# A decoder layer on one core: the product with the context is evicted by ScalarE, and a transfer adds the column sums, for seven of eight tiles

## The chip, the cores and the metric

The kernel runs on one core of one Trainium2 chip. The metric is the device time of an execution in microseconds (us). Times of the kernel before were taken in three runs; a further execution was recorded by the hardware profiler, and the views below are of that one. Engines are called as in the profile: PE is TensorE, DVE is VectorE, ACT is ScalarE, POOL is GpSimd, SP is SyncE.

## The reference, cut to what matters

One decoder layer works on 2 x 512 tokens of 1024 numbers: attention inside each token over 32 heads, a product with a context whose both sides are quantised to 256 levels, and a feed-forward part. After each comes an addition of its input and a layer norm.

```python
def _L0_xattn_ref(x1, x2, x1_scale, x1_zp, x2_scale, x2_zp):
    q1 = fake_quant(x1, x1_scale, x1_zp)   # (clip(round(x / s + z), 0, 255) - z) * s
    q2 = fake_quant(x2, x2_scale, x2_zp)
    return jnp.matmul(q1, q2)
...
x = _layernorm(x + _L0_attn_ref(x, Wq, bq, Wk, bk, Wv, bv))
x = _layernorm(x + _L0_xattn_ref(x, ctx_4096, x1_scale, x1_zp, x2_scale, x2_zp))
x = _layernorm(x + _L0_ffn_ref(x, ...))
```

## The kernel before

The 1024 tokens are eight tiles t = 0 to 7 of 128 tokens, one a partition; tile t's tokens lie in `xc` (128 x 1024, f32, in SBUF) and are changed in place. Tiles 0 to 3 use context 0, tiles 4 to 7 context 1. Two tiles make a block of the feed-forward part; blocks 0 and 1 go alone (`ffn`, products `pu` and `pl` at L827, then `pd` at L1057), blocks 2 and 3 together (`ffn_pair`, products `pp` at L942, then `ps` at L1317).

A tile goes through `scores` and `attend`: on DVE four products of 128 x 2048 (L474) with their reductions (L480), the exponentials on ACT (L493), four more products (L507) with reductions (L513), a scaling (L518) and the addition to the tokens with a row sum (L528). Then comes the layer norm. For seven tiles it is `normalise_aside`: ACT turns the row sum into minus the mean (`parts`, L346), takes the sum of squares (L351) and the variance (L353), POOL the reciprocal root `rstd` (L355), and ACT the shift (L359) and the result (L360). Tile 1 is the hurried one: its norms are on DVE (`normalise`: L324, L326, L328, L336) with the root on POOL (L330).

`cross(t, ...)` is the product with the context:

- ACT quantises the tokens in four passes (L375, L378, L381, L644) into `a`, in bf16 as whole numbers; the last pass also gives the row sum `total`. The temporary is `tmp` (tile `qt`, from the pool `work`, three buffers).
- The next tile's `scores` stand between ("between", L648). Then PE turns `a` round (`pta`, L652) and ACT copies it (`aT`, L653). For tile 1 DVE quantises (L364 to L366), and PE turns it at L630.
- Since the quantised numbers are stored from an offset, a row term `r` (from `total`) and a column term `crow` (from the context's column sums, made once a context by PE at L591 and ACT at L594) have to be added: DVE makes `r` (L658) and adds both to `xc` (L659).
- PE makes two products of 128 x 512 (`py`, L665) in two banks, and DVE adds each, scaled by `ns12`, to its half of `xc`, with a row sum (L670). In the up part of `ffn` and ahead of it `py` has banks of `ps_dn`, else of `ps_mm`.
- The layer norm follows, and `hand_over` turns `xc` round on PE (`pt_x`, L134) with copies by ACT (`x2T`, L135); then POOL's queue adds beta to `xc` with a transfer (L737).

Each engine does its instructions in a fixed order. The order comes from a scheduler that lays the steps of two generators (tokens and feed-forward) out with weights (`yield 3.5` and the like). `tc.issue_after(x)` keeps an instruction behind x in that order. `behind()` in `cross` puts DVE's instructions behind the lowering of the next tile's scores (`lowered`, L490), `behind_acted(True)` puts ACT's behind the last eviction of the feed-forward part (`acted`), and `behind_products()` PE's behind its last product (`lately`). `context_beside` quantises context 1 on ACT between the tiles (L375, L378, L577), from loads that POOL's queue issues (L558). In the up part a product `pu` lies in one of two banks of `ps_mm` until ACT has evicted it (L843, then L844), and `pl` likewise (L856, then DVE at L857).

Of the kernel before, what the change touches and what calls it, by code (L numbers as in the profile page):

```python
# [9 lines left out]
F32 = mybir.dt.float32  # L10
BF16 = mybir.dt.bfloat16
AF = mybir.ActivationFunctionType
ALU = mybir.AluOpType
# [3 lines left out]
P = 128  # L17
# [10 lines left out]
def kernel(  # L28
# [24 lines left out]
    nc = tc.nc  # L53
# [18 lines left out]
    HALF = 512  # L72
# [13 lines left out]
    small = ctx.enter_context(tc.tile_pool(name="small", bufs=3))  # L86
# [156 lines left out]
    for k in range(KE):  # L243

        pool, tag = (work, "work") if k % 3 == 0 else (xpool, "xc")
# [37 lines left out]
    with tc.issue_after(added[0].ins):  # L283
# [10 lines left out]
        ns12 = const.tile([P, 1], F32, name="ns12")  # L294
# [3 lines left out]
        s12d2 = const.tile([P, 1], F32, name="s12d2")  # L298
# [34 lines left out]
    def normalise(t, name):  # L333

        mean, rstd = mean_rstd([t[:, ts(h, HALF)] for h in range(E // HALF)], name)
        return nc.vector.tensor_scalar(t, t, mean, rstd, ALU.subtract, ALU.mult)  # L336

    def normalise_aside(t, sums, name):

        n = sums.shape[-1]  # L340
        parts = small.tile([P, 2], F32, tag="parts", name=f"parts_{name}")
        minus = parts[:, 0:1]
        if n > 1:
            minus = small.tile([P, 1], F32, tag="minus", name=f"minus_{name}")
        with behind_acted(True):
            nc.scalar.activation(  # L346
                parts[:, 0:n], sums, AF.Copy, scale=-1.0 / E, accum_out=minus if n > 1 else None
            )
        square = attp.tile([P, E], BF16, tag="square", name=f"square_{name}")
        total = small.tile([P, 1], F32, tag="square", name=f"squares_{name}")  # L350
        nc.scalar.activation(square, t, AF.Square, bias=minus, accum_out=total)  # L351
        ve = small.tile([P, 1], F32, tag="ve", name=f"ve_{name}")
        nc.scalar.activation(ve, total, AF.Identity, scale=1.0 / E, bias=eps)  # L353
        rstd = small.tile([P, 1], F32, tag="rstd", name=f"rstd_{name}")
        nc.gpsimd.tensor_tensor(rstd, ve, neg_half, ALU.pow)  # L355
        yield 3.0
        shift = small.tile([P, 1], F32, tag="shift", name=f"shift_{name}")
        with behind_acted(True):
            nc.scalar.activation(shift, rstd, AF.Identity, scale=minus)  # L359
        return nc.scalar.activation(t, t, AF.Identity, scale=rstd, bias=shift)  # L360

    def quantise(dst, src, tmp, rs, z):

        nc.vector.tensor_scalar(tmp, src, rs, z, ALU.mult, ALU.add)  # L364
        nc.vector.tensor_scalar(tmp, tmp, 0.0, QMAX, ALU.max, ALU.min)
        nc.vector.tensor_scalar(dst, tmp, ROUND, ROUND + CENTRE, ALU.add, ALU.subtract)  # L366

    acted = [None]

    def below_top(dst, src, tmp, rs, z):  # L370

        with behind_acted(dst is None):
            nc.scalar.activation(tmp, src, AF.Relu, scale=rs, bias=z)  # L375
        yield
        with behind_acted(dst is None):
            nc.scalar.activation(tmp, tmp, AF.Identity, bias=round_up)  # L378
        yield
        if dst is not None:  # L380
            nc.scalar.activation(dst, tmp, AF.Relu, scale=-1.0, bias=top_down)  # L381

    def behind_acted(pinned):

        if pinned and acted[0] is not None:
            return tc.issue_after(acted[0].ins)
        return ExitStack()
# [215 lines left out]
    tokens_added, routed = [None], [None]  # L603

    def spare_bank(name):

        if phase[0] in ("front", "up"):
            return ps_dn.tile([P, HALF], F32, tag="dn", name=name)
        return ps_mm.tile([P, HALF], F32, tag="mm", name=name)

    def behind_products():


        return tc.issue_after(lately[0].ins) if lately[0] is not None else ExitStack()

    def cross(t, xc, cq, crow, between):


        hurried = t == TB - 1
        tmp = work.tile([P, E], F32, tag="work", name=f"qt_{t}")  # L620
        a = attp.tile([P, E], BF16, tag="a", name=f"a_{t}")
        aT = tokp.tile([P, KC, P], BF16, tag="aT", name=f"aT_{t}")
        if hurried:

            quantise(a, xc, tmp, rs1, z1)
            yield 2.2
            pt = ps_tr.tile([P, KC, P], BF16, tag="tr", name=f"pta_{t}")
            with behind_products():
                for k in range(KC):
                    codes_turned[0] = nc.tensor.transpose(pt[:, k, :], a[:, ts(k, P)], identb)  # L630
            nc.scalar.copy(aT, pt)
            yield 1.0
            total = ps_tr.tile([P, 2], F32, tag="tr", name=f"pr_{t}")
            with tc.issue_after(expert[0].ins):
                for k in range(KC):
                    nc.tensor.matmul(
                        total, aT[:, k, :], onesb[:, 0:2], start=(k == 0), stop=(k == KC - 1)
                    )
            total = total[:, 0:1]
        else:  # L640
            total = small.tile([P, 1], F32, tag="total", name=f"total_{t}")
            for _ in below_top(tmp, xc, tmp, rs1, z1):
                pass
            nc.scalar.activation(  # L644
                a, tmp, AF.Identity, scale=-1.0, bias=code_down, accum_out=total
            )
            yield 2.0
            yield from between  # L648
            pt = ps_tr.tile([P, KC, P], BF16, tag="tr", name=f"pta_{t}")
            with behind_products():  # L650
                for k in range(KC):
                    nc.tensor.transpose(pt[:, k, :], a[:, ts(k, P)], identb)  # L652
            nc.scalar.copy(aT, pt)  # L653
            yield 4.0
        behind = ExitStack if hurried or t == NT - 1 else lambda: tc.issue_after(lowered[0].ins)
        r = small.tile([P, 1], F32, tag="r", name=f"r_{t}")
        with behind():
            nc.vector.tensor_mul(r, total, s12d2)  # L658
            nc.vector.scalar_tensor_tensor(xc, xc, r, crow, ALU.add, ALU.add)  # L659
        sums = small.tile([P, 2], F32, tag="sum2", name=f"sum2_{t}")  # L660
        for h in range(E // HALF):
            py = spare_bank(f"py_{t}_{h}")
            with behind_products():
                for k in range(KC):
                    crossed[t] = nc.tensor.matmul(  # L665
                        py, aT[:, k, :], cq[:, k, ts(h, HALF)], start=(k == 0), stop=(k == KC - 1)
                    )
            xh = xc[:, ts(h, HALF)]
            with behind():
                tokens_added[0] = nc.vector.scalar_tensor_tensor(  # L670
                    xh, py, ns12, xh, ALU.mult, ALU.add,
                    accum_out=None if hurried else sums[:, h : h + 1],
                )
        if hurried:
            last = normalise(xc, f"2_{t}")
            yield 6.0
        else:
            yield 3.0
            last = yield from normalise_aside(xc, sums, f"2_{t}")
            yield 6.0  # L680
        return last

    def token_path():
# [25 lines left out]
        for blk in range(NBLK):  # L709
            xcs = []  # L710
            x2T = []
            for i in range(TB):
# [9 lines left out]
                if t % (S // P) == 0:  # L722
# [3 lines left out]
                    batch = cqs[b], context_row(b, cqs[b])  # L726
                between = scores_left(t + 1) if t + 1 < NT else ()
                last = yield from cross(t, xc, *batch, between)

                def hand_over(blk=blk, t=t, i=i, xc=xc, x2T=x2T):  # L730
# [756 lines left out]
```

## Time and profile before

| what | before |
|---|---|
| median of three runs | 704.35 us (704.29 to 704.39) |
| the profiled execution | 704.49 us, of which the span from the first to the last instruction is 702.7 us |
| PE busy | 682.4 us, 97% of the span |
| DVE busy | 586.5 us, 83% |
| ACT busy | 261.8 us, 37% |
| POOL busy | 77.0 us, 11% |
| DMA engines, bytes moved | 139.08 MB, mean 198 GB/s |
| granted PE clock | 0.991 of full speed |

The page gives each engine's busy time, cuts the span into 40 slices (17.6 us each) with the busy share of each in tenths, and lists groups of instructions by line, engine, operation and tiles (written<-read), with their count, mean duration and what ended the idle time ahead of them. The view of waits says who waited for whom, in total, how often and longest. The view of one tile or line gives minimum, median and maximum durations in ns and the first and last start in us. The timeline lists instructions in order of time: start, duration, engine, line, operation, and in brackets the idle time ahead of it on its engine and what ended it. The chain of waits goes back from the last instruction to what released each step.

### The profile page before, as it was taken

Reading aid. Unit: us, or ns where it says so; the run is one execution under the profiler, and the core shown is the slowest. Engines: PE = TensorE matmul, PEld = TensorE weight load, DVE = VectorE, ACT = ScalarE, POOL = GpSimd, SP = SyncE. Lnnn points to the kernel's source line nnn. Section 1 sums busy time; section 2 is a strip of 40 time slices with the busy share of each in tenths; the row PEclk is TensorE's granted clock in tenths of the full one; section 3 lists DMA queues with packets and bytes.
Section 4 is the critical chain, followed back from the end, with each engine's and each line's share of the span. In section 5 each row is a group of like instructions: output and inputs, shape, how many; then the busy total and the mean of one; then the engine's idle time right before and its main releaser. Section 6 shows DMA issues by size and latency. Waiting matters only on the chain.

```text
span 702.7 us, 7462 instructions
## 1 busy us (share of the span) xinstructions
PE 682.4 (97%) x2812; PEld 482.6 (69%) x2812; DVE 586.5 (83%) x678; ACT 261.8 (37%) x440; POOL 77.0 (11%) x107
## 2 busy tenths in 40 slices
PE   8999999999999999999999999999999999999991
PEld 4666654578876444478876444488888888888881
DVE  5899987699999999799999950397787688897895
ACT  1287544222635458426736132212251200000252
POOL 1012112100011122001002000020010000001012
PEclk9999999999999999999999999999999999999996
DMA  9999528485446458446436534667897445556733
GB/s 336 304 346 370 127 32 290 116 288 175 135 132 174 178 194 254 134 166 215 145 119 177 182 120 126 238 194 242 338 344 254 164 166 171 168 197 192 207 84 120
DMA packets 70900, 139.08 MB, mean 198 GB/s; under 512 B 5264, under 2 KB 39696, under 8 KB 70864
## 3 DMA queue, kind: packets, MB, share of 16 engines
q1 hardware_dynamic: 60656, 106.87, 44.9%
q0 software_dynamic: 10064, 31.47, 16.3%
q8 instruction: 22, 0.36, 0.2%
q10 hardware_dynamic: 144, 0.26, 0.1%
q14 instruction: 14, 0.11, 0.0%
HBM read 114.99 MB, written 21.50 MB: 194 GB/s over the span
## 4 chain that ended last, share of the span: by engine, by line
PE 44%; issue 5%; ACT 3%; DVE 2%; POOL 1%; POOLq 0%
PE pd L1057 9%; PE pp L942 9%; PE ps L1317 7%; PE pp_mm L942 5%; PE pp_tr L942 4%; PE ps_mm L1317 4%; PE ps_tr L1317 3%; PE pu L827 2%; ACT square L351 1%; PE py L665 1%; POOL rstd L355 1%; DVE pav L507 1%; PE pl L827 1%; PE pt_x L134 0%; ACT xc L360 0%
## 5 line engine op out<-in xcount | busy, mean ns | idle before, releaser
L1057 PE MATMUL pd<-dn,h 128*128 128x512 f32 x320 | 139.3, 593 | 0.0
L827 PE MATMUL pu<-x2T,up 128*128 128x256 f32 x512 | 113.1, 380 | 0.8 <-ACT relu L843 0.8
L1057 PEld LDWEIGHTS pd<-dn,h 128*128 128x128 f32 x320 | 60.3, 190 | 71.8 <-issue 71.3
L827 PEld LDWEIGHTS pu<-x2T,up 128*128 128x128 f32 x512 | 96.4, 190 | 15.0 <-ACT relu L843 1.2
L507 DVE TENSOR_TENSOR pav<-s,v 128x2048 f32<-128x2048 f32 x32 | 72.5, 2282 | 0.0
L474 DVE TENSOR_TENSOR pqk<-qk 128x2048 f32<-128x2048 f32 x32 | 72.5, 2283 | 0.0
L480 DVE TENSOR_REDUCE s<-pqk 128x256 f32<-128x2048 f32 x32 | 72.3, 2278 | 0.1
L513 DVE TENSOR_REDUCE o<-pav 128x64 f32<-128x2048 f32 x32 | 72.0, 2266 | 0.0
L157 PE MATMUL pqk<-wqkv,xT 128*128 128x512 f32 x128 | 63.4, 595 | 1.2 <-DVE wqkv L249 0.9
L162 PEld LDWEIGHTS pv<-wqkv,xT 128*128 128x128 f32 x128 | 24.3, 190 | 24.2 <-issue 22.5
L355 POOL TENSOR_TENSOR rstd<-ve,neg_half 128x1 f32<-128x1 f32 x21 | 21.6, 1028 | 174.7 <-ACT ve L353 171.4
L162 PE MATMUL pv<-wqkv,xT 128*128 128x256 f32 x128 | 35.6, 379 | 0.0
L670 DVE SCALAR_TENSOR_TENSOR xc<-py,ns,xc 128x512 f32<-128x512 f32 x16 | 11.7, 743 | 26.4 <-PE py L665 26.4
L157 PEld LDWEIGHTS pqk<-wqkv,xT 128*128 128x128 f32 x128 | 23.6, 190 | 11.4 <-issue 4.3
L843 ACT ACTIVATE relu<-pu 128x256 f32<-128x256 f32 x32 | 12.1, 377 | 51.5 <-PE pu L827 51.5
L665 PE MATMUL py<-cq,aT 128*128 128x512 bf16 x128 | 28.9, 379 | 0.9 <-ACT aT L653 0.9
L1221 DVE TENSOR_TENSOR tt<-dn 128x1024 f32<-128x1024 f32 (+1 forms) x20 | 21.2, 1060 | 10.2 <-DMA dn<-in_L_ffn_down_w_dram 5.8
L458 PE MATMUL pe<-fc,exT 128*128 128x512 f32 x64 | 28.7, 594 | 0.0
L827 PE MATMUL pl<-x2T,fc 128*128 128x256 f32 x128 | 28.2, 380 | 0.5 <-ACT latent L856 0.5
L827 PEld LDWEIGHTS pl<-x2T,fc 128*128 128x128 f32 x128 | 24.2, 190 | 4.3 <-ACT latent L856 0.9
L665 PEld LDWEIGHTS <-aT 128*128 128x128 bf16 x128 | 12.4, 98 | 17.0 <-issue 2.0
L653 ACT COPY aT<-pta 128x1024 bf16<-128x1024 bf16 x7 | 7.0, 1007 | 43.9 <-PE pta L652 43.9
(311 smaller groups left out, 1165.5 us busy)
## 6 DMA issues: line engine op xcount, KB each, us to landing
up<-in_L_ffn_up_w_dram SPq DMA_DIRECT2D x16, 1024.0 KB, 5.5
dn<-in_L_ffn_down_w_dram SPq DMA_DIRECT2D x16, 1024.0 KB, 5.0
pair<-in_L_ffn_up_w_dram SPq DMA_DIRECT2D x8, 1024.0 KB, 6.3
dn<-tw SPq DMA_DIRECT2D x8, 1024.0 KB, 5.1
tw<-outer POOLq DMA_DIRECT2D x7, 1024.0 KB, 5.1
fc<-in_L_ffn_fc_w_dram SPq DMA_DIRECT2D x6, 1024.0 KB, 5.6
dn<-in_L_ffn_down_w_dram SPq DMA_DIRECT2D x12, 512.0 KB, 5.6
outer<-in_L_ffn_down_w_dram SPq DMA_DIRECT2D x5, 1024.0 KB, 5.1
```

Of the source, the lines that this page charges most:

```text
L157: projecting[0] = nc.tensor.matmul(pqk, xT[:, k, :], wqkv[k][:, 0 : 2 * DG], start=(k == 0), stop=(k == KE - 1))
L162: nc.tensor.matmul(pv[:, :DG], xT[:, k, :], wqkv[k][:, 2 * DG : 3 * DG], start=(k == 0), stop=(k == KE - 1),)
L458: expert[0] = nc.tensor.matmul(ps, exT[m // 2][:, m % 2, ts(l, P)], fc2[m // 2][:, m % 2, ts(n, HALF)], start=(m == 0), stop=(m == NL - 1),)
L474: nc.vector.tensor_tensor(prod.rearrange("p (d e g) -> p d e g", d=DC, g=G), q3[:, ts(c, DC), :].unsqueeze(2).to_broadcast([P, DC, D, G]), ...
L480: nc.vector.tensor_reduce(s[:, ts(c, DC), :].rearrange("p d e -> p (d e)"), prod.rearrange("p (c g) -> p c g", g=G), AX.X, ALU.add,)
L507: nc.vector.tensor_tensor(prod.rearrange("p (d g e) -> p d g e", d=DC, g=G), s[:, ts(c, DC), :].unsqueeze(2).to_broadcast([P, DC, G, D]), ...
L513: nc.vector.tensor_reduce(o[:, ts(c, DC), :].rearrange("p d g -> p (d g)"), prod.rearrange("p (c e) -> p c e", e=D), AX.X, ALU.add,)
L665: crossed[t] = nc.tensor.matmul(py, aT[:, k, :], cq[:, k, ts(h, HALF)], start=(k == 0), stop=(k == KC - 1))
L827: lately[0] = nc.tensor.matmul(ps[:, :NB], ws[:, k, wcols], xT[:, k, :], start=(k == 0), stop=(k == KE - 1))
L942: lately[0] = nc.tensor.matmul(banks[m], steps[g][m][:, k, :], moving[m][:, k, :], start=(k == 0 and m not in (6, 3, 7)), stop=(k == KH - ...
L1057: lately[0] = nc.tensor.matmul(pd[i][n], h[:, kk // 4, i, kk % 4, :], w[:, k, ts(n, HALF)], start=(kk == 0), stop=(kk == NK - 1),)
L1317: lately[0] = nc.tensor.matmul(banks[mm], unit(o, mm, j), inner_weights[o, cc][mm][:, j - lo, :], start=(j == 0 and mm not in FIRST_OF), s ...
```

## The change

For all tiles but tile 1 (seven of eight):

- `r` is made by ACT instead of DVE (an activation of 128 x 1 with `s12d2` as scale).
- The addition of `r` and `crow` by DVE is left out. `crow` is added to `xc` by a transfer that POOL's queue issues, from SBUF to SBUF with an addition.
- Each half of the product is evicted by ACT, which multiplies by `ns12` and adds `r`, into `tmp`; `tmp` is now held until the end of `cross`.
- DVE adds `tmp` to `xc` once, over all 1024 columns, with one row sum instead of two.

Tile 1 keeps its instructions. `normalise_aside` gets a sum of one column, and so takes the branch without `minus`.

```diff
-        with behind():
+        if hurried:
             nc.vector.tensor_mul(r, total, s12d2)
             nc.vector.scalar_tensor_tensor(xc, xc, r, crow, ALU.add, ALU.add)
-        sums = small.tile([P, 2], F32, tag="sum2", name=f"sum2_{t}")
+        else:
+            with behind_acted(True):
+                nc.scalar.activation(r, total, AF.Identity, scale=s12d2)
+            nc.gpsimd.dma_start(xc, crow, accum_op=ALU.add)
+        sums = small.tile([P, 1], F32, tag="sum2", name=f"sum2_{t}")
         for h in range(E // HALF):
...
             xh = xc[:, ts(h, HALF)]
+            if hurried:
+                tokens_added[0] = nc.vector.scalar_tensor_tensor(
+                    xh, py, ns12, xh, ALU.mult, ALU.add
+                )
+            else:
+                with behind_acted(True):
+                    acted[0] = nc.scalar.activation(
+                        tmp[:, ts(h, HALF)], py, AF.Identity, scale=ns12, bias=r
+                    )
+        if not hurried:
             with behind():
                 tokens_added[0] = nc.vector.scalar_tensor_tensor(
-                    xh, py, ns12, xh, ALU.mult, ALU.add,
-                    accum_out=None if hurried else sums[:, h : h + 1],
+                    xc, tmp, 1.0, xc, ALU.mult, ALU.add, accum_out=sums
                 )
```

## The prediction, on record before the changed kernel ran

> **What bounds the kernel now.** I read the slices of the page first, then what TensorE waited for, then the rows of the edited lines, then four places of the timeline.
>
> ```profile
> PE   8999999999999999999999999999999999999991
> DVE  5899987699999999799999950397787688897895
> ACT  1287544222635458426736132212251200000252
> ```
>
> TensorE (PE) is busy in every slice but the first and the last. VectorE (DVE) is nearly as full up to slice 23 (404 us) and loose after it; ScalarE (ACT) has room. The table by stage gives, from 140.5 to 404 us, PE 261.30, DVE 256.97 and ACT 126.42 of 263.50 us. So ACT can take work from DVE, but DVE time is worth only what it takes off PE's waits:
>
> ```profile
> PE py L665 <- ACT aT L653: 0.9, 1, 0.9
> PE pu L827 <- ACT relu L843: 0.8, 1, 0.8
> PE pt_x L134 <- ACT x2T L135: 0.7, 1, 0.7
> PE pl L827 <- ACT latent L856: 0.5, 1, 0.5
> ...
> PE pta L630 <- DVE a L366: 0.2, 1, 0.2
> ```
>
> (Total, times, longest.) These are all of PE's waits of weight behind 88 us. Measured from matmul start to matmul start in the timeline they are 1.03 us at 198.6, 0.98 at 323.2, 0.97 at 457.2, 0.68 at 373.0 and 0.41 at 122.5 (one of 0.48 at 103.5 lies ahead of the first edited addition). 4.1 us is all that the change could win there, and each us that PE waits anew is lost.
>
> **The change, part by part.** The rows:
>
> ```profile
> L659 DVE SCALAR_TENSOR_TENSOR xc<-xc,r,crow x8: 1269/1283/1286, 96.1 to 427.1; 128x1024 f32<-128x1024 f32 x8
> L670 DVE SCALAR_TENSOR_TENSOR xc<-py,ns,xc x16: 698/746/751, 113.9 to 451.7; 128x512 f32<-128x512 f32 x16
> L528 DVE SCALAR_TENSOR_TENSOR xc<-xc,o x7: 1209/1217/1224, 76.0 to 410.7; 128x1024 f32<-128x1024 f32 x7
> ...
> L594 ACT ACTIVATE crow<-pc,kd2s12d,ns12d x4: 758/778/792, 91.1 to 289.2; 128x512 f32<-128x512 f32 x4
> ```
>
> *DVE.* For each of seven tiles it loses L658 (0.15), L659 (1.28) and two L670 with their accumulator reads (about 1.5), and gains one addition of two 128x1024 SBUF operands with a row sum, of which L528 is the nearest row: 1.22 + 0.08. That is 1.6 us a tile, 11 us in all, none of it on PE.
>
> *ACT.* Two activations of 128x512 out of PSUM with scale and bias from columns, the form of L594: 0.78 each; r costs 0.29 (a 128x1 activation, as at L353); one sum for two saves 0.10 at L346 (parts to square 0.24 us at 77.3, 0.33 at 116.2). Some 1.75 us a tile, 12 us in all, on an engine at 48% of that stage. The first half is evicted while PE makes the second.
>
> [...]
>
> *The transfer.* Seven 512 KB additions from SBUF to SBUF on POOL's queue. Issue 0.87 to 0.89 us (L737, L1273); landing 4.8 us (L1273, the same form) to 14.7 us (the slowest transfer to any xc). It can start once ACT's first quantising pass has read xc, and the sum needs it 16 us later at the tightest (tile 2: 187 to 203 us; tile 7: 423 to 452). I take nothing. For tile 4 it waits for crow at 290 us; behind it in POOL's queue stands rstd_f, wanted at 299.8. The other reciprocal roots and qk fetches behind it have 4 us or more.
>
> *The wait that is added.* Before, the first half was added while PE made the second, and 0.8 us after PE's last product the tile was ready. Now DVE starts only when ACT has evicted the second half: 0.78 + 0.05 + 1.22 + 0.08. Behind it on DVE, ACT (parts, in order) and POOL (rstd) stands other work. The changed program's order on PE is the same up to 455 us, so I could follow these queues at each place:
>
> **A, tile 0 before tile 1 (122.5 us): +1.2.**
>
> ```profile
> 115.41 0.75 DVE L670 SCALAR_TENSOR_TENSOR xc<-py,ns,xc 128x512 f32<-128x512 f32 x1 [0.79 <-PE py L665]
> ...
> 119.31 0.81 DVE L336 TENSOR_SCALAR xc<-xc,mv,rstd 128x1024 f32<-128x1024 f32 x1 [3.08 <-POOL rstd L330]
> ```
>
> Tile 1 is the hurried one, but its rstd stands on POOL behind tile 0's, and tile 0's waits for ACT's square of tile 0, for the sum. That sum now ends at 115.41 + 0.78 + 0.05 + 1.30 = 117.5 instead of 116.2; less 0.10 at parts, L336 and the quantising start 1.2 later, and so does pta (L630), for which PE waits already. Nothing covers it.
>
> **B, tile 3 (264.1 us): +1.2.** Here DVE is full. The sum moves behind one more reduction (2.20, L513) but costs 1.23 instead of 1.42 and DVE is 0.57 ahead: at tiles 2 and 3 without L658 and L659 it goes on 0.19 earlier each (they filled a wait for ACT's exponentials, 196.3 to 197.4 and 241.0 to 242.1, which stays), and tile 2's addition gave 0.19 (two steps of 0.67 against 1.15). 2.20 - 0.19 - 0.57 = 1.44 later. ACT waits in order at parts, so square, rstd and xc (L360, ends 263.88) follow; PE takes up pt_x at 264.10 without a wait, 0.16 us to spare. Bounds 0 (a wait for a ctx load, 0.22 and more, hides part) and 1.4.
>
> **C, tile 4 (323.2 us): +1.2, from -0.1 to +2.5.** This is the wait of 0.98 in the table:
>
> ```profile
> 315.10 0.30 ACT parts L346 x2
> ...
> 322.88 0.28 ACT relu L843
> 323.15 0.04 issue
> ```
>
> ACT's parts of tile 4 stands ahead of the relu that frees PE's bank. The sum goes behind a reduction, a product and a scaling (2.20 + 2.29 + 0.34 = 4.83); against it stand 0.19, the removed L659 (1.2) and DVE's lead at that point: 0.9 to 2.3, since tile 5's exponentials now stand ahead of two of tile 4's quantising passes on ACT (285.7 or 287.1 instead of 288.0, by whether ACT has made up B's delay). So it is 1.1 to 2.5 later, and PE is late by B's 1.2 already: -0.1 to +1.3. The block's own rstd is then issued about 321 to 322 us, when DVE is inside a 128x2048 product. Reciprocal roots that begin inside such a product take 1.85 to 2.44 us (L355 at 207.2, 227.9, 259.0, 275.6), 0.55 else: up to +1.2. I take the middle.
>
> [...]
>
> **D, tile 5 (373.0 us): -0.7 (0 to -0.7).** On DVE tile 5's sum gets a product, L528 and a reduction more in front (2.20 + 1.15 + 2.20) and costs 0.48 more itself; DVE's lead (2.3 at tile 6's exponentials, 1.2 for L659, 0.67 for the first half) is 4.2 against it: 1.9 later. PE is 2.4 late by then, so the wait for latent (0.68), which comes behind that sum on ACT, goes.
>
> **E, tile 7 into the pair stage (457.2 us): +0.1 (0 to +0.4).** Tile 7's xc is 1.7 us later (0.78 + 0.05 + 0.5, and an x2T copy of 0.57 now ahead of it on ACT, less 0.1), but the new order puts the 16 gate products (about 1 us) and a pair product (0.43) ahead of pt_x on PE: it would be free at 457.4 and gets xc at 458.5, a wait of 1.1 instead of 0.97.
>
> Sum: 1.2 + 1.2 + 1.2 - 0.7 + 0.1 = 3.0 us. The profiled execution took 704.49 us (span 702.7); 707.5 by it. The median shown is 704.35, so I predict **707.35 us**, 0.43% slower. About 0.2%, 1.4 us, is what can be told from no change.
>
> **Rivals.**
> 1. *Faster.* DVE's 11 us come early enough that the waits at 323.2 and 373.0 vanish and A and B stay covered: -1.7, 702.7 us. For it: DVE is full just there. It decides if ACT gets the sum no later than before; but A has no cover, and DVE already stands idle there for 3.08 us, waiting for POOL. 5%.
> 2. *Little.* A holds, but B is hidden by ACT's waits for loads, C lands at its low end and D gives 0.7 back: 1.2 + 0 - 0.1 - 0.7 = 0.4, 704.8 us. 11%.
> 3. *The transfer is late.* It needs a landing of over 16 us, against 4.8 to 14.7; at 20 us tile 2's to 4's sums would each wait some 4 us, and of that perhaps 6 in all would reach PE: 713 us. 4%.
> 4. *The change doesn't do what it says* (ACT as the bound): at 48% of its stage it would have to cost twice its rows. 1%, with 2's price.
>
> **Numbers.** The forecast has 79%. Its own ends are A 1.2 + B 0.3 + C -0.1 + D -0.7, 0.7 us (705.05), and A 1.2 + B 1.4 + C 2.5 + E 0.4 + D -0.3, 5.2 us (709.55). The range 704.8 to 709.5 takes in rivals 2 and 4 and leaves out 1 and 3, with the forecast's thin ends some 15%. Slower by over 0.2% (705.76 and up): the forecast less its lowest part (5%), and rival 3: 78%. Within 0.2%: that part with rivals 2 and 4, 17%. Faster by over 0.2%: rival 1, 5%.
>
> **What would show it.** A: pta at L630 waits over 1.5 us on PE. B: a new PE wait of about 1 us at tile 3's pt_x, near 266 us. C: the wait for relu grows to 2 us or so. D: the wait for latent is gone. DVE's busy time falls by 11 us, ACT's rises by about 12. It would be wrong if PE shows waits for the transfer, or if rstd falls between the products and C is nothing.

## The result and the profile after

The changed kernel took **709.61 us** (median of 4, 708.80 to 711.27) where the kernel before took 704.37 beside it: a ratio of 1.0063, 95% interval 1.0046 to 1.0080. The ratios in this document are taken over the fast runs and are not the quotients of the medians beside them. Two more sets of executions, on two chips, gave 1.0054 (1.0036 to 1.0073) and 1.0074 (1.0054 to 1.0095). The prediction was 707.35, from 704.8 to 709.5: the direction is right, the size too small, the first median just above the range. By the ratio, the 704.35 us from which the forecast was made become 708.8, inside it.

The profiled execution is the shortest of the four: 708.80 us, span 707.0, against 704.49 and 702.7. Its slices of 17.7 us, to be held against the three shown in the prediction:

```profile
PE   8999999999999999999999999999999999999991
DVE  5899985699999999899899910198687688897895
ACT  1288544222646459436636134222251200000252
```

PE stays full. DVE's busy time fell from 586.5 to 575.1 us (11.4; predicted 11) and ACT's rose from 261.8 to 273.2 (11.4; predicted 12): the work moved as priced. The groups of the two new instructions (count, then minimum, median and maximum in ns):

```profile
L679 ACT ACTIVATE qt<-py,r,ns x14: 777/777/780, 114.1 to 455.3; 128x512 f32<-128x512 f32 x14
...
L684 DVE SCALAR_TENSOR_TENSOR xc<-qt,xc x7: 1209/1223/1226, 116.5 to 456.1; 128x1024 f32<-128x1024 f32 x7
```

They cost what L594 and L528 cost before (0.778 and 1.217). The loss is in what PE waits for:

```profile
PE pta L630 <- DVE a L366: 2.2, 1, 2.2
PE pu L840 <- ACT relu L856: 1.6, 1, 1.6
...
PE pt_x L134 <- ACT xc L360: 1.3, 2, 0.7
...
PE py L669 <- ACT aT L653: 0.8, 1, 0.8
```

The wait for tile 1's codes (L630) and the one for the relu have grown, tile 3's pt_x is a new one, the wait for latent is gone. Measured from matmul start to matmul start less the usual step, in all profiles of the study (us; "relu" is the wait near 325 us, "pair" the pt_x near 460 us; pauses of 0.4 to 0.7 us near 166 us in own_buffer_tile1, tile0_before, transfer_alone and tile4_before, and of 0.2 to 0.3 us near 355 us, are not in it):

| kernel | L630 | py, 200 | pt_x, tile 3 | relu | latent | pair |
|---|---|---|---|---|---|---|
| before | 0.41 | 1.03 | 0 | 0.98 | 0.68 | 0.97 |
| changed, first profile | 2.33 | 0.96 | 0.86 | 1.80 | 0 | 0.76 |
| changed, second | 1.95 | 1.01 | 0.85 | 1.38 | 0 | 0.77 |
| changed, third | 2.25 + 1.70 at half clock | 1.02 | 0.86 | 1.39 | 0 | 0.77 |
| own_tile | 1.68 | 1.25 | 0.86 | 1.56 | 0 | 0.76 |
| own_buffer_tile1 | 1.67 | 0.49 | 0.86 | 1.80 | 0 | 0.76 |
| tile0_before | 0.41 | 0.63 | 0.85 | 1.38 | 0 | 0.77 |
| no_transfer | 2.21 | 1.04 | 0.86 | 1.95 | 0 | 0.75 |
| no_transfer_again | 1.94 | 1.02 | 0.86 | 1.67 | 0 | 0.74 |
| transfer_alone | 0.41 | 0.78 | 2.04 | 0 | 0 | 0.98 |
| late_transfer | 0.41 | 1.01 | 0 | 1.96 | 0 | 0.99 |
| tile3_before | 1.72 | 1.01 | 2.01 | 1.98 | 0 | 0.77 |
| tile4_before | 4.40 + 2.54 at half clock | 0.31 | 0.86 | 0 | 0 | 0.76 |
| tiles04_before | 0.42 | 0.85 | 0.86 | 0 | 0 | 0.77 |

From before to the first profile that is +1.92 - 0.07 + 0.86 + 0.82 - 0.68, with 0.28 for a new pause of PE at 355.5 us that I did not follow, and at the pair stage -0.21 and +0.18 for a new pause just ahead of it: 3.1 us. PE was 0.31 us late already at 103 us, ahead of any edited addition (a wait for the projections' weights, 1.4 where it was 0.9), and its last matmul comes 3.39 us later. The span grew by 4.3: 0.9 us more lies behind the last matmul.

### The profile page after: what moved, and what is told of

Read it like the earlier page. It is cut to its first block, busy times and chain, and to the rows that moved or that the text cites. A ratio compares the mean times of both kernels' runs of the same rounds, so it can differ in the third digit from the quotient of the medians.

```text
span 707.0 us, 7473 instructions
## 1 busy us (share of the span) xinstructions
PE 682.4 (97%) x2812; PEld 482.1 (68%) x2812; DVE 575.1 (81%) x650; ACT 273.2 (39%) x454; POOL 85.8 (12%) x114
## 4 chain that ended last, share of the span: by engine, by line
PE 60%; DVE 23%; ACT 7%; DMA 5%; issue 3%; POOL 1%; SPq 0%; POOLq 0%; DVEq 0%; ACTq 0%
PE pd L1070 9%; PE pp L955 9%; PE pqk L157 8%; PE ps L1330 5%; PE pu L840 5%; PE pp_mm L955 5%; DVE pav L507 4%; PE pv L162 4%; DVE s L480 4%; DVE pqk L474 4%; PE pp_tr L955 4%; DVE o L513 4%; PE ps_mm L1330 2%; PE py L669 2%; PE pl L840 2%
## 5 line engine op out<-in xcount | busy, mean ns | idle before, releaser
L474 DVE TENSOR_TENSOR pqk<-qk 128x2048 f32<-128x2048 f32 x32 | 72.6, 2286 | 0.0
L480 DVE TENSOR_REDUCE s<-pqk 128x256 f32<-128x2048 f32 x32 | 72.4, 2281 | 0.1
L507 DVE TENSOR_TENSOR pav<-s,v 128x2048 f32<-128x2048 f32 x32 | 72.4, 2283 | 0.0
L513 DVE TENSOR_REDUCE o<-pav 128x64 f32<-128x2048 f32 x32 | 72.0, 2268 | 0.0
L684 DVE SCALAR_TENSOR_TENSOR xc<-qt,xc 128x1024 f32<-128x1024 f32 x7 | 8.6, 1222 | 50.4 <-ACT qt L679 50.4
L355 POOL TENSOR_TENSOR rstd<-ve,neg_half 128x1 f32<-128x1 f32 x21 | 23.1, 1101 | 168.1 <-ACT ve L353 164.8
```

Source lines behind the costliest of these rows:

```text
L474: nc.vector.tensor_tensor(prod.rearrange("p (d e g) -> p d e g", d=DC, g=G), q3[:, ts(c, DC), :].unsqueeze(2).to_broadcast([P, DC, D, G]), ...
L480: nc.vector.tensor_reduce(s[:, ts(c, DC), :].rearrange("p d e -> p (d e)"), prod.rearrange("p (c g) -> p c g", g=G), AX.X, ALU.add,)
L507: nc.vector.tensor_tensor(prod.rearrange("p (d g e) -> p d g e", d=DC, g=G), s[:, ts(c, DC), :].unsqueeze(2).to_broadcast([P, DC, G, D]), ...
L513: nc.vector.tensor_reduce(o[:, ts(c, DC), :].rearrange("p d g -> p (d g)"), prod.rearrange("p (c e) -> p c e", e=D), AX.X, ALU.add,)
```

## The experiments

Two theories went in. *Mine*, after the first profile: late sums at tiles 0, 3 and 4 cost what the table shows, a part of L630 is something I had not priced, and the transfers are free. *The rivals*: the losses at PE only take each other's place (undo one and another grows), or the transfers cost.

### A buffer that is given back late

In the first profile of the changed kernel, DVE's timeline between tile 0's sum and tile 1's codes (start, duration, then in brackets the idle time ahead and what ended it):

```profile
120.82 0.81 DVE L336 TENSOR_SCALAR xc<-xc,mv,rstd 128x1024 f32<-128x1024 f32 x1 [2.98 <-POOL rstd L330]
122.33 0.81 DVE L364 TENSOR_SCALAR qt<-xc,rs,z 128x1024 f32<-128x1024 f32 x1 [0.69 <-DMA e<-e]
```

L336 comes 1.51 us later than before (119.31, shown in the prediction), 0.31 of it from the start of the program: 1.2, as predicted. But the quantiser L364 now stands 0.69 us more, for a transfer of `e`. In the kernel before it followed L336 without a gap:

```profile
120.16 0.81 DVE L364 TENSOR_SCALAR qt<-xc,rs,z 128x1024 f32<-128x1024 f32 x1
```

The temporary `qt_0` is held until ScalarE's evictions are added, so tile 1's quantiser is given another of the pool's three buffers: the one from which the first 128 rows of the experts' product (L464) are still being written to DRAM. The stretches around it (length, busy time and count of each engine, then PE's granted clock, the busy share of the DMA engines and GB/s) go with a late landing:

```profile
113.20:118.00 4.80, 4.80 (x18) 2.27 (x17) 1.30 (x3) 1.74 (x3) 0.49 (x1) 1.00 1.02 410
118.00:122.30 4.30, 4.30 (x11) 1.71 (x9) 0.81 (x1) 3.56 (x7) 1.09 (x2) 1.00 0.59 235
```

The write is issued at 113.16, while weights, tokens and context loads issued just ahead of it fill the DMA engines at 410 GB/s, and lands 9.07 us later; the next such write, at 123.48, takes 2.94. In the kernel before the first one takes 9.08 us too, but there nothing waits for it. Taking the wait away was tried twice, with a tile for the eviction and with one for tile 1's quantiser:

```diff
-                        tmp[:, ts(h, HALF)], py, AF.Identity, scale=ns12, bias=r
+                        ev[:, ts(h, HALF)], py, AF.Identity, scale=ns12, bias=r
...
-                    xc, tmp, 1.0, xc, ALU.mult, ALU.add, accum_out=sums
+                    xc, ev, 1.0, xc, ALU.mult, ALU.add, accum_out=sums
```

> The changed kernel, but ScalarE evicts the products into a tile of their own instead of the quantiser's temporary, so that this one is free again when the last quantising pass has read it. Theory (the wait at tile 1's transposes is 1.2 us of a longer chain plus 0.7 us of a buffer: tile 1's quantiser, L364, gets a buffer whose transfer of expert rows to DRAM has not landed): L364 follows L336 without idle time, PE's wait at L630 falls from 2.2 to about 1.5 us, time 708.9 us against the 709.6 of the changed kernel, and its spread over the runs shrinks. Rival (the whole wait is the longer chain, or the transfers): no change at L630, 709.6.

Measured: 707.44 us against 705.21 before, 1.0045 (1.0018 to 1.0071), from 706.83 to 715.61. L630 fell to 1.68 and L364 follows L336. The spread did not shrink: three of the twelve executions took over 711 us, and the profiled one, 715.61, holds a wait of 5.9 us at 518 us, far behind L630. It is for a load of `pair` weights that SP issued at 506.54, where the changed kernel's first profile has 501.45; why it came later was not followed.

```diff
-        tmp = work.tile([P, E], F32, tag="work", name=f"qt_{t}")
+        if hurried:
+            tmp = tokp.tile([P, E], F32, tag="qt1", name="qt_1")
+        else:
+            tmp = work.tile([P, E], F32, tag="work", name=f"qt_{t}")
```

> The changed kernel, but tile 1's quantiser gets a buffer of its own, in place of the one from which the first rows of experts are still being written to DRAM; every engine's order is the same but for one load that SP issues three places earlier at 515 us. Theory (this landing is a wait of its own at L364): L364 follows L336 without idle time, PE's wait at L630 is 1.5 us in the profile, the median is 0.7 to 1.5 us under that of the changed kernel beside it, and what is left is 2.2 us over the kernel before. Rival (the landing costs only in the profiles that happened to show it): the same median as the changed kernel, within 0.4 us.

> The changed kernel a third time, as the base for the three kernels run beside it. Theory (3 us of PE waits plus a landing that tile 1's quantiser waits for and that comes 0 to 2.7 us late): ratio to the kernel before 1.004 to 1.006. Rival (the change costs only what its quietest profile shows, 2.2 us): 1.003.

On one chip the changed kernel took 709.79 us (708.57 to 713.00), with a buffer of its own for tile 1 707.64 (707.02 to 707.87), the kernel before 704.96: ratios 1.0074 and 1.0034 (1.0021 to 1.0046). More than the expected 0.7 to 1.5 us is gone, and the spread with it. DVE in the profile with the own buffer:

```profile
120.55 0.81 DVE L336 TENSOR_SCALAR xc<-xc,mv,rstd 128x1024 f32<-128x1024 f32 x1 [2.98 <-POOL rstd L330]
121.40 0.81 DVE L364 TENSOR_SCALAR qt<-xc,rs,z 128x1024 f32<-128x1024 f32 x1
```

L630 waits 1.67, 1.26 more than before: the longer chain alone.

How a landing that is 0.3 to 0.7 us late can cost 2 us is seen in the changed kernel's third profile, in its stretches behind L630 (columns as above):

```profile
124.00:125.00 1.00, 0.95 (x9) 0.71 (x10) 0.00 (x0) 0.30 (x1) 0.00 (x0) 0.92 1.02 414
125.00:128.40 3.40, 3.40 (x5) 1.35 (x4) 0.00 (x0) 0.72 (x1) 0.00 (x0) 0.52 0.08 33
128.40:131.00 2.60, 2.60 (x18) 1.19 (x17) 0.90 (x2) 0.58 (x1) 0.00 (x0) 1.00 0.00 0
```

PE had stood idle for 2.09 us, and then its granted clock is 0.52 for 3.4 us. Over these matmuls PE's delay against the kernel before grows from 1.56 to 3.26 us: 1.70 us more. The first profile has nearly the same wait, 2.16 us, without it. What decides whether the half clock follows such a wait is not shown by these runs.

How often it happens can be read from the granted clock that is on record for each execution. The eleven profiles without a stretch of half clock between 20 and 690 us have a mean clock of 0.991 to 0.993, the three with one (changed, third; own_tile; tile4_before) 0.985 to 0.989. Of the changed kernel's 16 executions nine lie at 0.990 or less (709.3 to 713.0 us; the other seven took 707.2 to 710.0). With the buffer of its own it is none of 6, for the kernel before, in its executions beside the experiments, 11 of 81. By this the half clock belongs to the cost in over half of the changed kernel's executions; where in the program it fell, only the profiles show.

### Undoing tiles one at a time

One edit makes all of these: for the tiles of a set, `cross` keeps the instructions of the kernel before.

```diff
-        if hurried:
+        kept = t in {0}
+        if hurried or kept:
+            with behind():
                 nc.vector.tensor_mul(r, total, s12d2)
                 nc.vector.scalar_tensor_tensor(xc, xc, r, crow, ALU.add, ALU.add)
```

(and likewise at the evictions and the last addition; `sums` has two columns for a kept tile).

> The changed kernel, but tile 0 keeps the instructions of the kernel before (VectorE adds column sums and both products); tiles 2 to 7 are as changed. Theory (a wait ahead of 123 us is paid in full at the end): PE's wait at L630 is back at 0.2 to 0.4 us, time 707.7 us. Rival (what PE loses at L630 only takes the place of later waits for VectorE): the waits at tile 3's pt_x and for the relu at 327 us grow by what L630 gives back, 709 to 709.6 us.

706.48 us against 705.21, 1.0011 (0.9998 to 1.0024). L630 is back at 0.41, and neither tile 3's pt_x (0.85) nor the relu (1.38) grows: what PE loses at tile 0 is not made good later. The rival falls.

> The changed kernel once more, so that the kernels of this study have it beside them on one chip, with a second profile. Theory (what the first profile shows is what the change costs: 3.1 us of PE waits): the ratio to the kernel before is 1.004 to 1.005, and the same PE waits come back: 2.2 at L630, 1.6 for the relu, 0.7 twice at pt_x. Rival (the executions longer than the profiled one have a further loss that the first profile doesn't show): the ratio stays at 1.006 or more, and a PE wait appears that isn't in the list.

708.81 us against 704.87, with the waits of the table. Its profile is the shortest execution, 707.21 us, in which L364 stands 0.31 us for the landing. The ratio is a little above the theory's 1.004 to 1.005; the half clock told of above may be why: this profile has none, but two of the six executions have a granted clock of 0.989 and 0.990.

> The changed kernel, but tile 3 keeps the instructions of the kernel before. Theory (tile 3's sum goes behind one more reduction on VectorE, and PE waits 0.86 us for its norm at pt_x): this wait is gone; the one for the relu at 327 us, which hangs on VectorE and not on PE, takes part of it back; 0.4 us less than the changed kernel (0 to 0.9). Rival (tile 3's norm is late from the reciprocal root that POOL takes 1.95 us over beside a VectorE product, whoever adds): the wait stays at 0.6 us or more, time as the changed kernel.

708.98 us, 1.0061 (1.0042 to 1.0080): no gain, and the wait at tile 3's pt_x rose to 2.01. My theory of this place falls. What sets it is the reciprocal root. In this kernel:

```profile
261.19 2.28 DVE L474 TENSOR_TENSOR pqk<-qk 128x2048 f32<-128x2048 f32 x1
261.27 2.63 POOL L355 TENSOR_TENSOR rstd<-ve,neg_half 128x1 f32<-128x1 f32 x1
```

and in the changed kernel:

```profile
261.84 2.29 DVE L474 TENSOR_TENSOR pqk<-qk 128x2048 f32<-128x2048 f32 x1
262.61 1.95 POOL L355 TENSOR_TENSOR rstd<-ve,neg_half 128x1 f32<-128x1 f32 x1 [0.78 <-ACT ve L353]
...
267.19 0.98 PE L134 MATMUL pt_x<-ident,xc 128*128 128x128 f32 x7 [0.70 <-ACT xc L360]
```

Both roots end 0.43 us after the DVE product in which they began (263.47 and 263.90; 264.13 and 264.56). In the kernel before, the root began earlier in a product and ended at 260.88, again 0.43 behind that product's end (260.45):

```profile
258.17 2.28 DVE L507 TENSOR_TENSOR pav<-s,v 128x2048 f32<-128x2048 f32 x1
259.03 1.85 POOL L355 TENSOR_TENSOR rstd<-ve,neg_half 128x1 f32<-128x1 f32 x1 [0.78 <-ACT ve L353]
```

So the norm does not move with the sum but in steps of a product: with tile 3's old instructions the sum ends 2.85 us earlier than in the changed kernel (256.88 against 259.73; 1.02 of that because PE is less late here), but ACT's order has one more pass of the context (L577, 1.14 us) ahead of the variance, the root begins 0.08 us after a product has begun, and 2.63 us go by. All 29 roots at L355 that lasted over 0.9 us in the profiles of before, the changed kernel and this one began inside a two-operand DVE instruction; 28 ended 0.41 to 0.43 us after that one, and the last lay over three in a row and ended 0.42 after the third. The other 40 take 0.54 to 0.65, one 0.83.

> The changed kernel, but tile 4 keeps the instructions of the kernel before. Theory (the wait for the relu is tile 4's late sum and a reciprocal root of 2.1 us beside a VectorE product): the wait at 327 us falls from 1.8 to 0.5 us or less, and the wait for latent at 377 us stays away; 1.0 us less than the changed kernel (0.3 to 1.6). Rival (VectorE is late by then from tile 3 and before, and tile 4's addition of the column sums comes on top): 1.8 us or more, time not less.

706.08 us against 704.87, 1.0031 (1.0009 to 1.0052); the middle of its executions lies 2.7 us under the changed kernel beside it (708.81). The wait for the relu is gone, and latent's stays away: confirmed. The gain is larger than expected, and than the 1.4 to 1.8 us of that wait; the rest is not accounted for. The profiled execution is its longest, 713.62 us: 2.85 us of it are lost ahead of 13 us, and it shows the landing at its worst. On DVE:

```profile
123.37 0.81 DVE L336 TENSOR_SCALAR xc<-xc,mv,rstd 128x1024 f32<-128x1024 f32 x1 [2.98 <-POOL rstd L330]
126.94 0.81 DVE L364 TENSOR_SCALAR qt<-xc,rs,z 128x1024 f32<-128x1024 f32 x1 [2.76 <-DMA e<-e]
```

L464's row lands after 11.1 us there, PE stands 4.23 us until 129.34, and its granted clock is 0.50 until 134.7 (columns as above):

```profile
128.00:131.00 3.00, 1.66 (x9) 1.28 (x10) 1.18 (x2) 0.59 (x1) 0.00 (x0) 0.50 0.14 57
131.00:134.70 3.70, 3.70 (x6) 1.51 (x5) 0.00 (x0) 0.42 (x1) 0.00 (x0) 0.50 0.00 0
```

Five matmuls take 0.85 to 0.96 us instead of 0.43, and PE loses 2.54 us by it.

### The transfer

```diff
-            nc.gpsimd.dma_start(xc, crow, accum_op=ALU.add)
```

> The changed kernel without the seven transfers; it leaves the column sums of the context out for seven tiles. Nothing else differs in any engine's order. Theory (the transfers are hidden and nothing waits for them): 709.6 us, within 0.2, with the same PE waits. Rival (the 3.7 MB they add delay other transfers or hold VectorE or GpSimd at SBUF): 708.5 us or less, and the landing at 122.3 us that tile 1's quantiser waits for comes earlier.

> The changed kernel without the seven transfers, which leaves the column sums of the context out for seven tiles, now beside the changed kernel on one chip. Theory (the transfers cost nothing): the same median as the changed kernel beside it, within 0.5 us. Rival (the ratio of 1.0021 that it had on another chip, against 1.0054 and 1.0063 of the changed kernel, was the transfers' doing): 1.5 to 3 us under it.

707.31 us (1.0021, 1.0009 to 1.0032) on one chip, and 706.71 (1.0033, 1.0017 to 1.0048) beside 709.79 on another: 3 us less, so the theory that they cost nothing falls. No wait of PE or DVE is for them, and the landing that L364 waits for does not come sooner without them, as the rival had it (8.85 and 8.69 us after its issue, against 9.07, 8.69 and 9.00). In the changed kernel they land as fast as predicted:

```profile
L663 POOL DMA_DIRECT2D xc<-crow x7: 855/899/922, 93.4 to 428.3; - x7
...
DMA to landing us min/median/max: 5.1/6.4/8.9
```

One part of the cost is at the very end. POOL's queue closes with a drain, and the end of the span follows it by 0.8 us, while the last transfer landed 2.3 us (before) and 2.9 us (after) ahead of the drain's end. Before and after (minimum, median and maximum in ns):

```profile
L1482 POOLq DRAIN  x3: 46/108/6324, 695.6 to 702.4; - x3
```

```profile
L1495 POOLq DRAIN  x3: 46/99/6896, 699.3 to 706.7; - x3
```

It takes 6.32 or 6.33 us without the transfers (both profiles of this experiment too), 6.65 with four, 6.73 with five, 6.81 with six and 6.89 or 6.90 with seven: 0.08 us for each that the queue has issued, 0.57 in all. The other 2.5 us are not settled. No PE wait in the profiles accounts for them: the second profile of this experiment and the changed kernel's second have the same wait at L630 (1.94 and 1.95), and PE's last matmul comes 0.36 us apart, as far as PE was apart at 103 us already (0.37). What differs is the half clock: a granted clock of 0.990 or less stands in 3 of the 24 executions without the transfers, against 9 of 16 with them. So it was met less often; that the transfers bring it about, and by what, is not shown.

The transfer alone, in the kernel before:

```diff
-        with behind():
+        if hurried:
             nc.vector.tensor_mul(r, total, s12d2)
             nc.vector.scalar_tensor_tensor(xc, xc, r, crow, ALU.add, ALU.add)
+        else:
+            nc.gpsimd.dma_start(xc, crow, accum_op=ALU.add)
```

> The kernel before with the transfer alone: for seven tiles the column sums are added by the transfer, VectorE adds the two halves of the product from PSUM as before, and the row term r is left out of these tiles (it adds one number to all columns of a token, which the layer norm that follows takes away). VectorE loses 1.43 us a tile and ScalarE gains nothing. Theory (the late sum behind ScalarE's eviction is what costs, the transfer is free): no new PE wait, those for the relu at 323 us and for the latent at 373 us shrink, 703.4 us (702.7 to 704.4). Rival (the transfer or its place on the queue costs): 706 us or more.

> The kernel before with the transfer alone, as in the run of that name, but for tiles 4 to 7 only (row term r left out there, which the norm takes away); tiles 0 to 3 as before. Theory (the transfer alone takes the waits for the relu and for the latent, and its loss at tile 3's pt_x comes from a new order there, which tiles 4 to 7 don't touch): all PE waits as before but for those at 323 and 373 us, which go; 702.7 us where the kernel before takes 704.4, a ratio of 0.9976. Rival (PE's waits move on to the next place where VectorE or ScalarE is late): 0.999 to 1.001.

For seven tiles 705.83 us against 705.21, 1.0005 (0.9990 to 1.0020); for tiles 4 to 7 705.92 against 704.87, 1.0015 (1.0002 to 1.0028). Both expectations of a gain fall, and so does "no new PE wait". DVE was relieved (577.1 us busy instead of 586.5 in the first), and the waits for the relu and for latent went there; but tile 3's root began 0.08 us after a product had begun, took 2.64 us and cost 2.04. In the second, tile 3 shows no wait, as expected, but the planner used the freed time to put a product of the next tile (L474) ahead of tile 4's sum, which ended at 315.69 instead of 315.06, and the wait for the relu rose to 1.96. In these two, DVE's time bought nothing.

### A version with fewer tiles changed

> The changed kernel, but tiles 0 and 4 keep the instructions of the kernel before; the change is left for tiles 2, 3, 5, 6 and 7. Theory (the change costs at tile 0 and tile 4, and gives at tile 5): PE waits 0.4 at L630, 0.6 at py, 0.85 at tile 3's pt_x, none for the relu at 325 us nor for latent, 1.1 at the pair stage: 2.95 us against the 4.07 of the kernel before, 703.8 us where that takes 704.9, ratio 0.9984. Rival (the planner's new order makes another root or eviction late): 1.000 to 1.003.

704.14 us (703.84 to 705.79) against 704.96: 0.9986 (0.9976 to 0.9997), as expected, on one chip and with an interval that just leaves out no change; the changed kernel beside them took 709.79. PE's longest waits are now:

```profile
PE pt_x L134 <- ACT xc L360: 1.3, 2, 0.7
PE pqk L157 <- DVE wqkv L249: 1.2, 1, 1.2
...
PE py L671 <- ACT aT L654: 0.7, 1, 0.7
```

With tile 0 kept, tile 1's quantiser has its old buffer back as well, so the landing is out of the way (L364 follows L336 at 0.04 us), and none of the twelve executions has a granted clock under 0.991.

## Why the prediction was right or wrong

- **A, tile 0 before tile 1: +1.2 by the chain, which is 1.26 in the kernel with an own buffer and 1.20 at L336.** Right in size. What failed is the step that was not there: the change holds the temporary until the end of `cross`, the text of the change says so, and I priced nothing for it. That buffer's successor waits for a DRAM write: 0.31 to 0.69 us in the changed kernel's three profiles, 2.76 in another kernel's. Behind PE waits of 2.09 and 4.23 us a half clock followed that cost 1.70 and 2.54 us. With a buffer of its own for tile 1 the median falls by 2.15 us (709.79 to 707.64), nearly as much as the prediction was short by (709.61 against 707.35).
- **B, tile 3: +1.2; measured +0.86.** The sum does come later, 3.68 us in the profile, 2.23 of them PE's own lateness: 1.45, where the working gave 1.44. The root's end moved by the same 3.68. ACT took 0.42 of it back: its next step (shift, L359) began 0.55 us behind the root's end before, behind passes of the context, and 0.13 now; the wait of 0.22 for a context load, which the prediction names with its lower bound, stood there. With PE's 0.16 to spare that leaves 0.87. So the working holds here, with 0.3 too much at its end; but it took the norm to move with the sum, and the norm moves by products of DVE: the old instructions in the same place cost 2.01.
- **C, tile 4: +1.2 from -0.1 to +2.5; measured +0.4 to +0.8** in the three profiles. The sum ends at 317.84 instead of 315.06, and the block's own root takes 2.12 us from 321.94 on, inside a product, as bounded. Undoing tile 4 takes the whole wait away.
- **D, latent: -0.7; measured -0.68.** It stays away in every variant.
- **E, pair stage: +0.1; measured 0.0** (PE is 3.37 us late ahead of it and 3.38 behind it).
- **The transfer: "I take nothing". It cost 0.57 us**, not at its landing, which is as predicted, but in the drain of POOL's queue, of which I had not thought. Without the transfers the medians lie 3 us lower in all; the other 2.5 us stay open. Rival 3 (a late landing) did not occur.
- **The old addition read PSUM, the new one SBUF alone**: no root ran while an L684 did in the first profile, so what L684 does to a root is not shown. The long roots on PE's path began inside products (L474, at 262.61 and 321.94), as at 259.03 before (L507). Three roots that began inside an addition with one operand in PSUM (L1347 and L1350 before, L1363 in the changed kernel) took 0.55 to 0.56 us.

The sum of 3.0 us against 3.1 us of PE waits in the first profile is thus partly luck: A too small by 0.7, B and C too large by 0.3 and 0.4. To these come 0.57 for the drain and, by the granted clock in nine of 16 executions, the half clock.

## What to carry to other kernels

When an edit keeps a temporary longer, list the pool's tenants in order: someone else gets the next buffer, and waits for whatever its tenant still does; here a write to DRAM behind loads, for 0.31 to 2.76 us. Moving the eviction to an idle engine lengthened tile 0's chain by 1.26 us although it took 11.4 us off the full engine, so move one only for the tiles whose result nobody waits for: the same change was 0.5 to 0.7% slower for seven tiles and 0.14% faster for five. And where a small POOL instruction stands on the path beside DVE products, look where in a product it begins: tile 3's sum 2.85 us earlier left PE a wait of 2.01 us where it had 0.86.

## What the runs showed of the hardware

- A 128x1 root on POOL that began inside a two-operand DVE product ended 0.41 to 0.43 us after that product, at whatever point it began, and so took up to 2.66 us instead of 0.55 (three profiles). Roots that began inside a reduction (L480, L513) took 0.56 us.
- A wait of PE of 2.09 us was followed by 3.4 us at a granted clock of 0.52, one of 2.16 us was not. Around the end of one of 4.23 us, and of one of 5.9 us, the clock was 0.50 for some 6.8 us (127.9 to 134.7 in tile4_before, 514.7 to 521.6 in own_tile).
- Each transfer that POOL's queue issued lengthened its closing drain by 0.08 us (6.32 with none of the seven to 6.89 with all).
